# Query order, masks, mixing factors and due offsets in a fused attention and MLP block on one core

## The chip, the core and the metric

The kernel runs on one core of a Trainium2 chip. The time is the device time of one execution in microseconds. The core has five engines that each work through a queue of their own in program order: PE (matrix multiply, with its weight loads shown apart as PEld), DVE (vector), ACT (scalar and activation), POOL (general) and SP, which issues the DMAs here. The engines wait for each other through semaphores.

## The reference

The input has 8 batches of 512 tokens of width 256. Two layers are computed. The first adds an attention and an FP4-quantised MLP to the tokens, both fed with the normalised tokens; the second adds a gated recurrence with its own small MLP and an INT4 linear layer. The change lies in the attention of the first layer, which is, for each of 16 heads of width 64 with 64 memory keys ahead of the 512 keys of the batch:

```python
dots = jnp.einsum('bhid,bhjd->bhij', q, k) * SCALE
dots = jnp.einsum('bhij,hk->bkij', dots, pre_proj)      # heads are mixed before the softmax
dots = jnp.where(causal[None, None], mask_value, dots)
kth = jax.lax.top_k(dots, TOPK)[0][..., -1:]             # TOPK = 64
dots = jnp.where(dots < kth, mask_value, dots)
attn = jax.nn.softmax(dots, axis=-1)
attn = jnp.einsum('bhij,hk->bkij', attn, post_proj)      # and after it
out = jnp.einsum('bhij,bhjd->bhid', attn, v)
```

Everything is fp32.

## The kernel before, in words

The program has three stages. **Preparation** transposes and quantises weights. **Attention** then works through 64 groups: 8 batches of 8 groups of 64 queries. The last part of it also runs the MLP of batch 0 and the quantising of batch 1 (`early_mlp`, `begin_last`). The **second phase** runs the MLP of the other batches and the second layer.

A group g of a batch holds 8 blocks of 8 queries, and a block lies in SBUF with 128 partitions (16 heads by 8 queries) and as many columns as it may see keys, 72 to 576. Groups are taken in the order 7, 0, 5, 2, 6, 1, 4, 3, and two successive groups share one set of queries. The steps of a group are:

- `queries` (L1020), once for a pair: PE multiplies the query weights with the normalised tokens (L1032), four 128 x 128 products to a PSUM bank, each as two passes, so that a half of the pair shows as 16 matmuls. ACT evicts the bank (L1040) and sorts the queries by block on the way, with a write pattern whose neighbouring elements lie four apart.
- `scores` (L1049): in two halves of four blocks each, PE makes raw scores per head (L1066, tiles of 64 x 32), ACT copies them out (L1081), SP issues four DMAs (L1088) that spread them from rows of queries to blocks of heads, PE mixes the heads with the constant `blend` (L1101), ACT takes the exponential (L1109). POOL then multiplies the last 64 columns of all eight blocks with a prepared 0/1 array `reach` (L1118).
- `search` (L1255) finds the 64th largest value of each row by counting: five rounds of eight counts, on ACT (L1144) or DVE (L1148, L1150), and a small step between rounds (`narrow`, L1162) on POOL or DVE. The tables `LONG`, `EDGE` (first two groups) and `LAST` (last four groups) say for each round how many of the eight counts go to ACT and whether the step runs on POOL.
- `soften` (L1294): DVE takes the eight largest below the threshold (L1214, L1217), picks the value (L1221 to L1228) and zeroes what is smaller (L1241). `mixers` (L1318): POOL multiplies the constant `mix` with the reciprocal row sums in two products of 512 elements (L1330).
- `attend` (L1338): PE turns the rows and mixes heads (L1373, L1353), ACT evicts (L1379), PE multiplies with the values (L1397), ACT evicts (L1412). `project_out` (L1418) follows for each pair.

Scores live in one ring of 16,896 columns. `room` (L1445) cuts it into three levels of 5,632; a pair fills a level, one group from its start, one from its end. Six groups are in flight.

The order of work is written out by a planner (`Plan`, L97). Every step is added with an engine, an assumed cost, its dependencies and the buffers that it takes. Each gets a due time from the table `DUE` (L62), as an offset in groups from its own group's place on a nominal clock. `Plan.run` (L130) simulates the engines with the assumed costs and, among steps that could start at about the same moment on an engine, issues the one that is due first. The resulting order is fixed in the program; the chip keeps it per engine, whatever the real durations are. `MLP_DUE` and `BEGIN_DUE` place the early MLP and the early quantising relative to the last group.

In the second phase, tiles live in 16 pieces of 1,024 columns of the ring, listed by number (L1741 to L1744). A branch with an exact version of the attention (L1692) follows the attention and is not taken with these inputs.

Of the kernel before, what the change touches and what calls it, by code (L numbers as in the profile page):

```python
# [32 lines left out]
ORDER = (7, 0, 5, 2, 6, 1, 4, 3)  # L33

RING = 3 * 5632
PACE = 33.0
LEVEL = GB * (WD[0] + WD[-1])
# [12 lines left out]
LAST = ((GB, True),) * 2 + ((GB // 2, False),) * 2 + ((0, False),)  # L50
# [9 lines left out]
MLP_DUE = (-3.18, 3.76)  # L60
BEGIN_DUE = (1.83, 3.43)
DUE = dict(  # L62
    tokens=((-5.94, 2.79),),
    keys=((-7.0, -2.2),),
    queries=((-2.66, -2.56),),
    scores=((-0.82, 0.09), (-0.22, -0.17),),
    search=((2.83, 3.39), (2.51, 3.02),),
    soften=((-1.53, 4.19), (-4.65, -2.79),),
    values=((1.38, 4.78),),
    attend=((5.21, 5.55), (2.0, 2.47),),  # L70
    project=((0.38, 3.82),),
# [560 lines left out]
def block_kernel(ctx: ExitStack, tc: tile.TileContext, a: dict, out: bass.AP):  # L632
# [44 lines left out]
    xqT_1 = piece(15).rearrange("p (e n) -> p e n", e=DC)  # L677
# [3 lines left out]
    with ExitStack() as c0:  # L681
# [16 lines left out]
        reach = keep.tile([P, GB, GR], F32, name="reach")  # L698
# [17 lines left out]
        with tc.tile_pool(name="prep", bufs=1) as prep, tc.tile_pool(name="prep_ps", bufs=1, space=PSUM) as pps:  # L716
# [140 lines left out]
            r.gpsimd.memset(reach, 0.0)  # L857
            for i in range(GB):
                if i:
                    r.gpsimd.memset(reach[:, i, : i * RB], 1.0)  # L860
                r.vector.tensor_scalar(reach[:, i, i * RB : (i + 1) * RB], cmask, -1.0, 1.0, ALU.mult, ALU.add)
# [9 lines left out]
            for c0_, c1_ in ((8192 + DC * 2 * FI, 12288), (12288 + 3 * FI + FKC * D, RING)):  # L871
                r.gpsimd.memset(ring[:, c0_:c1_], 0.0)
# [121 lines left out]
        def keys_of(pl, o, xdone):  # L994
# [3 lines left out]
            for rnd in range(2):  # L998
                for h in range(2):
                    for c in (4 * rnd, 4 * rnd + 2):  # L1000
# [15 lines left out]
                        op = pl.add("PE", 1.9, mm, xdone, ["ps_m"] + ([f"k{rnd}"] if h == 0 and c == 4 * rnd else []), after=[op])  # L1016
# [3 lines left out]
        def queries(pl, pair, o, xdone):  # L1020
# [3 lines left out]
            lo, hi = sorted(pair)  # L1024
            for c0_ in range(0, HC, 4):
                def mm(c0_=c0_):
                    if c0_ == 0:
                        q["T"] = qp_.tile([P, HC, 2, GR], F32, name="qT")
                    q["pq", c0_] = ps = ps_m.tile([P, 512], F32, name="ps_mi")
                    for j in range(4):  # L1030
                        for e in range(DC):
                            nc.tensor.matmul(  # L1032
                                ps[:, j * P : (j + 1) * P].rearrange("p (g i) -> p g i", g=2),
                                wqT[:, e, (c0_ + j) * P : (c0_ + j + 1) * P],
                                o["xnT"][:, e].rearrange("p (g i) -> p g i", i=GR)[:, lo : hi + 1 : hi - lo],
                                start=(e == 0), stop=(e == DC - 1),
                            )

                def evict(c0_=c0_):
                    nc.scalar.copy(  # L1040
                        q["T"][:, c0_ : c0_ + 4].rearrange("p c g (s i b) -> p (c g s) b i", s=2, i=RB),
                        q.pop(("pq", c0_)).rearrange("p (u b i) -> p u b i", b=4, i=RB),
                    )
# [5 lines left out]
        def scores(pl, g, s, q, kdone, qdone, wait=(), free=(), plain=False):  # L1049

            done, raws, op = [], [], None
            side = side_of(g)
            home = pl.add("none", 0.0, lambda: None, wait)
            for sub in range(GR // SUB):
                nk = MEM + g * GR + (sub + 1) * SUB
                k, wires = {}, []
                for rnd in range(2):
                    got = []
                    parts = [(0, nk)] if nk <= 512 else [(0, nk // 2), (nk // 2, nk)]
                    for n0, n1 in parts:  # L1060
                        def mm(rnd=rnd, n0=n0, n1=n1, sub=sub, k=k):
                            k["of", rnd, n0] = some = [ps_m.tile([P, 512], F32, name="ps_mi") for _ in range(2)]
                            for j in range(4):
                                for u in range(2):
# [3 lines left out]
                                        q["T"][rows, 4 * rnd + j, side, sub * SUB : (sub + 1) * SUB],  # L1068
# [4 lines left out]
                            "PE", 0.2 + 0.00166 * (n1 - n0), mm, kdone[rnd] + qdone, ["ps_m"] * 2,  # L1073
# [3 lines left out]
                        for u in range(2):  # L1077
# [5 lines left out]
                            got.append(pl.add("ACT", 0.12 + 0.00083 * (n1 - n0), evict, [op], ["raw"] if n0 == 0 else [], ["ps_m"]))  # L1083
                    for u in range(2):
                        t = 2 * rnd + u

                        def spread(t=t, nk=nk, sub=sub, k=k):
                            nc.sync.dma_start(s[t * SUB : (t + 1) * SUB, 4 * sub : 4 * sub + 4, :nk], k["raw", t][:, :nk])  # L1088
# [3 lines left out]
                        wires.append(pl.add(f"lat{t}", 2.0, lambda: None, [wire], (), ["raw"]))  # L1092
                op2 = None
                for b in range(4 * sub, 4 * sub + 4):
# [11 lines left out]
                    op2 = pl.add("PE", 0.06 * len(cols) + 0.00166 * n, mm, wires, ["ps_s"] * len(cols), after=[op2])  # L1106
                    for i, (n0, n1) in enumerate(cols):
# [5 lines left out]
                        done.append(pl.add("ACT", 0.12 + 0.00083 * (n1 - n0), evict, [op2], (), ["ps_s"]))  # L1113

            def mask():

                at = MEM + g * GR
                nc.gpsimd.tensor_tensor(s[:, :, at:], s[:, :, at:], reach, ALU.mult)  # L1118
                if plain:
                    step = WD[g] + RB  # L1120
                    flat = s.rearrange("p b w -> p (b w)")
                    new = flat[:, at : at + (GB - 1) * step].rearrange("p (b w) -> p b w", w=step)[:, :, :RB]
                    nc.gpsimd.tensor_tensor(new, new, cmask.unsqueeze(1).to_broadcast([P, GB - 1, RB]), ALU.add)
                    new = s[:, GB - 1, WD[g] - RB :]
                    nc.gpsimd.tensor_tensor(new, new, cmask, ALU.add)

            return [pl.add("POOL", 1.1, mask, done)], raws

        def side_of(g):

            return int(g > NG - 1 - g)
# [186 lines left out]
        def mixers(pl, den, w, op=None):  # L1318
# [8 lines left out]
            for j in range(2):  # L1327
                def make(j=j):
                    w["mix"][j] = m = rp.tile([P, 4, P], F32, name="mixd")
                    nc.gpsimd.tensor_tensor(  # L1330
                        m, mix.rearrange("p k i -> p (k i)").unsqueeze(1).to_broadcast([P, 4, P]),
                        w["rden"][:, 4 * j : 4 * j + 4].unsqueeze(2).to_broadcast([P, 4, P]), ALU.mult,
                    )

                done.append(pl.add("POOL", 1.2, make, [op], ["rp"]))
            return done

        def attend(pl, g, s, w, yt, deps, vdone):  # L1338
# [5 lines left out]
            for c, (col, n) in enumerate(chunks):  # L1344
# [22 lines left out]
                for j in range(2 if n == P else 0):  # L1367
# [10 lines left out]
                    def evict(c=c, n=n, j=j):  # L1378
# [6 lines left out]
                        "PE", 0.96, turn, [deps[j]], ["ps_a"] + (["at"] if j == 0 else []),  # L1385
# [5 lines left out]
                def mm(c=c, n=n, last=last):  # L1391
# [12 lines left out]
                    "PE", 1.1, mm, got + vdone, ["ps_y"] if c == 0 else [], ["at"], after=[summed]  # L1404
                )
            side = side_of(g)
            w["turned"] = turned

            def out():
                if side:  # L1410
# [5 lines left out]
            return [pl.add("ACT", 0.5, out, [summed], ["y"] if side else [], ["ps_y"])]  # L1416

        def project_out(pl, dst, pair, yt, deps):  # L1418
# [5 lines left out]
            def add():  # L1424
                out_ = wp.tile([P, D], F32, name="o", bufs=1)
                nc.vector.tensor_tensor(out_, yt.pop("po"), bout, ALU.add)
                for g in pair:
                    nc.sync.dma_start(dst(g), out_[side_of(g) * GR : (side_of(g) + 1) * GR, :])

            op = pl.add("PE", 3.55, mm, deps, ["ps_m"], ["y"])  # L1430
# [14 lines left out]
        def room(n):  # L1445
            g = ORDER[n % NG]
            at = n // 2 % 3 * LEVEL + (LEVEL - GB * WD[g]) * (n % 2)
# [110 lines left out]
        def begin_last(pl, guard, ready):  # L1558
# [4 lines left out]
            def keep_():  # L1563
                nc.sync.dma_start(xq_d, piece(15))
# [10 lines left out]
        groups = [(b, g) for b in range(B) for g in ORDER]  # L1575
# [14 lines left out]

        used = 2 * LEVEL

# [14 lines left out]
        yt, ydone, judged, freed = {}, [], [None, None], []  # L1607
        for n, (b, g) in enumerate(groups):
            if g == ORDER[0]:
# [8 lines left out]
            if n % 2 == 0:  # L1618
                pair = ORDER[n % NG : n % NG + 2]
# [4 lines left out]
            s = room(n)  # L1624
            last = g == ORDER[-1]
# [338 lines left out]
```

## Time and profile before

| | us |
|---|---|
| median of 3 runs (lowest, highest) | 2479.11 (2475.32, 2479.76) |
| the profiled execution | 2485.27 |
| its span | 2483.6 |
| PE busy in the span | 2184.8 |
| DVE busy | 2100.5 |
| ACT busy | 1903.0 |
| POOL busy | 1083.7 |

Busy is the time in which an engine runs an instruction. A group of the profile is written as line, engine, operation, output and inputs with their sizes, then after a bar the busy time in us, the mean duration of one in ns, and the idle time of the engine before them with what ended it. Successive records of one engine may overlap by about 0.1 us, as the end of a matmul or an ACT instruction reaches into the next. In the rows of 40 slices a digit is the busy share of a slice of 62 us in tenths.

### The profile page before, as it was taken

The page shows a single profiled execution, that of the slowest core. Times are in us where ns is not written, and L with a number is a line of the kernel's source. Part 1 is how long each engine was busy: PE and PEld are TensorE (multiplying, and loading weights), DVE is VectorE, ACT ScalarE, POOL GpSimd, SP SyncE. Part 2 cuts the span into 40 slices and gives each one's busy share as a digit, 9 for nine tenths or more (in the row PEclk, how much of TensorE's full clock was granted, in tenths as well). Part 3 has the DMA queues.
Part 4 walks back from the last instruction along what each step waited for, and adds up shares of the span by engine and source line. Part 5 has one row for each costly group of instructions (what it writes and reads, how often), then busy time and mean ns, then how long its engine had stood idle before and what let it go on. Part 6 is the DMA issues. An engine that isn't in the chain of part 4 may idle for free. (4 is left out here: it accounts for less than half of the span.)

```text
span 2483.6 us, 56595 instructions
## 1 busy us (share of the span) xinstructions
PE 2184.8 (88%) x19593; PEld 1546.0 (62%) x19593; DVE 2100.5 (85%) x6550; ACT 1903.0 (77%) x5426; POOL 1083.7 (44%) x2007
## 2 busy tenths in 40 slices
PE   5887999999999998999999999999466789989997
PEld 4544765777677676676767667666355456666654
DVE  8658889998999998999989998899997788777762
ACT  3389989989999999999999999899733446443442
POOL 5103536445454553554545455454424544444330
PEclk8897999999999999999999999999787889999998
DMA  6252242234233225323332422442000310000000
GB/s 221 57 102 44 55 67 47 59 57 71 55 53 70 48 55 78 55 60 57 64 56 48 80 48 61 66 86 64 3 16 16 113 34 25 19 9 18 0 9 17
DMA packets 112222, 134.35 MB, mean 54 GB/s; under 512 B 19356, under 2 KB 97975, under 8 KB 111415
## 3 DMA queue, kind: packets, MB, share of 16 engines
q1 hardware_dynamic: 111926, 130.65, 25.7%
q8 instruction: 156, 2.56, 0.5%
q14 instruction: 140, 1.14, 0.2%
HBM read 27.32 MB, written 15.73 MB: 17 GB/s over the span
## 5 line engine op out<-in xcount | busy, mean ns | idle before, releaser
L1144 ACT ACTIVATE junk<-ring,cur 128x328 int8<-128x328 f32 (+22 forms) x1520 | 856.0, 573 | 10.0 <-POOL cur L1206 5.4
L1148 DVE TENSOR_SCALAR_CACHE_REDUCE junk<-ring,cur 128x520 int8<-128x520 f32 (+7 forms) x976 | 509.1, 540 | 60.7 <-POOL cur L1206 51.3
L1373 PE MATMUL ps_at<-mixd,ring 128*128 128x128 f32 x2560 | 358.6, 291 | 72.4 <-POOL mixd L1330 66.2
L1373 PEld LDWEIGHTS ps_at<-mixd,ring 128*128 128x128 f32 x2560 | 320.9, 200 | 110.5 <-POOL mixd L1330 74.2
L1101 PE MATMUL ps_sc<-ring,blend 128*128 128x276 f32 (+49 forms) x1152 | 358.8, 432 | 24.1 <-DMA ring<-raw 15.1
L1214 DVE SCALAR_TENSOR_TENSOR y<-ring,cur 128x520 f32<-128x520 f32 (+56 forms) x512 | 323.3, 631 | 6.2
L1144 ACT ACTIVATION_READ_ACCUMULATOR junk<-ring,cur 128x1 f32 x1520 | 311.1, 205 | 0.0
L1241 DVE SCALAR_TENSOR_TENSOR ring<-ring,kth 128x520 f32<-128x520 f32 (+56 forms) x512 | 294.0, 582 | 0.9
L1101 PEld LDWEIGHTS ps_sc<-ring,blend 128*128 128x128 f32 x1152 | 191.8, 192 | 155.9 <-ACT ring L1109 73.3
L1160 POOL TENSOR_TENSOR cur<-base,raw 128x8 f32<-128x8 f32 x182 | 44.2, 243 | 537.1 <-ACT junk L1144 508.7
L1217 DVE MAX8 top<-y 128x8 f32<-128x520 f32 (+56 forms) x512 | 255.7, 499 | 17.6
L1109 ACT ACTIVATE ring<-ps_sc 128x280 f32<-128x280 f32 (+33 forms) x576 | 223.5, 416 | 26.7 <-PE ps_sc L1101 20.5
L1397 PE MATMUL ps_y<-at,v 128*64 128x64 f32 (+1 forms) x6144 | 221.3, 225 | 25.5 <-ACT at L1379 19.2
L1397 PEld LDWEIGHTS ps_y<-at,v 128*64 128x64 f32 (+1 forms) x6144 | 196.1, 138 | 74.6 <-ACT at L1379 40.2
L1081 ACT COPY raw<-ps_mi 128x288 f32<-128x288 f32 (+14 forms) x576 | 217.0, 415 | 29.5 <-DMA ring<-raw 19.0
L1066 PE MATMUL ps_mi<-kt,qT 64*32 64x288 f32 (+14 forms) x4608 | 227.1, 428 | 12.3 <-ACT raw L1081 11.4
L1379 ACT COPY at<-ps_at 128x512 f32<-128x512 f32 x320 | 188.9, 595 | 38.6 <-PE ps_at L1373 36.3
L1196 POOL TENSOR_TENSOR by<-gap,minus 128x8 f32<-128x8 f32 x120 | 204.9, 1707 | 9.4
L1330 POOL TENSOR_TENSOR mixd<-mix,rden 128x512 f32<-128x512 f32 x128 | 142.6, 1129 | 101.4 <-DVE rden L1322 49.2
L1118 POOL TENSOR_TENSOR ring<-ring,reach 128x512 f32<-128x512 f32 x64 | 86.4, 1350 | 197.6 <-ACT ring L1109 113.0
L260 PE MATMUL ps_gu<-big,ring 128*128 128x352 f32 x448 | 149.7, 480 | 16.6 <-DVE hid L260 10.3
L1422 PE MATMUL ps_mi<-woT,y 128*128 128x256 f32 x512 | 131.0, 414 | 16.2 <-ACT y L1412 16.2
(308 smaller groups left out, 3954.7 us busy)
## 6 DMA issues: line engine op xcount, KB each, us to landing
ring<-raw SPq DMA_DIRECT2D x32, 288.0 KB
ring<-raw SPq DMA_DIRECT2D x32, 272.0 KB
ring<-raw SPq DMA_DIRECT2D x32, 256.0 KB
ring<-raw SPq DMA_DIRECT2D x32, 240.0 KB
ring<-raw SPq DMA_DIRECT2D x32, 224.0 KB
ring<-raw SPq DMA_DIRECT2D x32, 208.0 KB
ring<-raw SPq DMA_DIRECT2D x32, 192.0 KB
ring<-raw SPq DMA_DIRECT2D x32, 176.0 KB
```

The lines of the kernel that those rows point to most:

```text
L1066: nc.tensor.matmul(some[u][j * SUB : (j + 1) * SUB, : n1 - n0], q["T"][rows, 4 * rnd + j, side, sub * SUB : (sub + 1) * SUB], kt[rows, 4 * ...
L1081: nc.scalar.copy(k["raw", 2 * rnd + u][:, n0:n1], k["of", rnd, n0][u][:, : n1 - n0])
L1101: nc.tensor.matmul(ps[:, : n1 - n0], blend.rearrange("p k i -> p (k i)"), s[:, b, n0:n1], start=True, stop=True,)
L1109: nc.scalar.activation(s[:, b, n0:n1], k["pb", b][i][:, : n1 - n0], AF.Copy if plain else AF.Exp, scale=DH ** -0.5)
L1144: nc.scalar.activation(junk, src, AF.Sign, bias=thr, scale=-1.0, accum_out=raw[:, b : b + 1])
L1148: nc.vector.tensor_scalar(junk, src, thr, 0.0, ALU.is_ge, ALU.add, accum_out=raw[:, b : b + 1])
L1196: eng.tensor_tensor(by, gap[:, 1], minus, ALU.pow)
L1214: nc.vector.scalar_tensor_tensor(y, src, cur[:, 0, b : b + 1], src, ALU.is_lt, ALU.mult)
L1217: nc.vector.max(out=top[:, b, 1:], in_=y)
L1241: nc.vector.scalar_tensor_tensor(src, src, kth[:, b : b + 1], e, ALU.is_ge, ALU.mult, accum_out=den[:, b : b + 1])
L1373: nc.tensor.matmul(pt[:n, b * P : (b + 1) * P], s[:, 4 * j + b, col : col + n], w["mix"][j][:, b, :], start=True, stop=True,)
L1397: nc.tensor.matmul(w["py"][j * DH : (j + 1) * DH, q * GR : (q + 1) * GR], vs[c][:n, k * DH : (k + 1) * DH], ats[c][:n, k, :], start=(c == ...
```

## The change

- **Queries.** The moving operand of L1032 is read query by query across the blocks, with a step of 8 columns, so the PSUM bank already holds the sorted order and the eviction is a plain copy.
- **Halves.** The first half of a group's scores takes blocks 0, 2, 4, 6 and the second 1, 3, 5, 7, so the first half is 24 columns wider than before. The query weights of the raw scores are read with a step of 2.
- **Masks.** `reach` is gone. For each half POOL clears the columns behind each block's last key with memsets (four and three), once the DMAs have landed, and after the exponentials multiplies only the 8 newest columns of the blocks by an 8-column array `below` (two products). The memsets of unused parts of the ring in the preparation go.
- **Mixing factors.** The two products of 512 elements become four of 256.
- **Ring.** `places` lays groups first in, first out, and lists for each group the earlier ones that it overlaps; those are waited for.
- **Planner.** All due offsets change, and several assumed costs.
- **Last groups.** `LAST` gives all counts of rounds three and four to ACT, and the step after round three to POOL.
- **Later pieces.** The pieces of the second phase are numbered by when the last groups free them, and the early quantising waits for the groups that lie where it writes.

```diff
+ORDERS = (ORDER,) * B
-LEVEL = GB * (WD[0] + WD[-1])
+SCRATCH = 11264
+def places(order):
+    at, found, held = 0, [], [(-1, SCRATCH, RING)]
+    for n, g in enumerate(order):
+        size = GB * WD[g]
+        if at + size > RING:
+            at = 0
+        found.append((at, [m for m, c0, c1 in held if c0 < at + size and at < c1]))
+        held = [(m, c0, c1) for m, c0, c1 in held if not (at <= c0 and c1 <= at + size)] + [(n, at, at + size)]
+        at += size
+    return found, held
-LAST = ((GB, True),) * 2 + ((GB // 2, False),) * 2 + ((0, False),)
+LAST = ((GB, True),) * 3 + ((GB, False), (0, False))
-MLP_DUE = (-3.18, 3.76)
-BEGIN_DUE = (1.83, 3.43)
+MLP_DUE = (-5.1, -4.84)
+BEGIN_DUE = (-0.86, 4.46)
 DUE = dict(
-    tokens=((-5.94, 2.79),),
-    keys=((-7.0, -2.2),),
-    queries=((-2.66, -2.56),),
-    scores=((-0.82, 0.09), (-0.22, -0.17),),
-    search=((2.83, 3.39), (2.51, 3.02),),
-    soften=((-1.53, 4.19), (-4.65, -2.79),),
-    values=((1.38, 4.78),),
-    attend=((5.21, 5.55), (2.0, 2.47),),
-    project=((0.38, 3.82),),
+    tokens=((-6.23, -2.15),),
+    keys=((-3.1, 0.28),),
+    queries=((-1.77, -0.35),),
+    scores=((-0.29, 0.89), (0.36, 0.78),),
+    search=((2.42, 5.15), (3.63, 5.17),),
+    soften=((1.27, 3.95), (0.74, 2.19),),
+    values=((4.79, 5.02),),
+    attend=((6.0, 6.0), (-2.66, 5.66),),
+    project=((-3.36, 2.98),),
...
@@ queries
                             nc.tensor.matmul(
-                                ps[:, j * P : (j + 1) * P].rearrange("p (g i) -> p g i", g=2),
-                                wqT[:, e, (c0_ + j) * P : (c0_ + j + 1) * P],
-                                o["xnT"][:, e].rearrange("p (g i) -> p g i", i=GR)[:, lo : hi + 1 : hi - lo],
+                                ps[:, j * P : (j + 1) * P], wqT[:, e, (c0_ + j) * P : (c0_ + j + 1) * P],
+                                o["xnT"][:, e].rearrange("p (g b i) -> p g i b", b=GB, i=RB)[:, lo : hi + 1 : hi - lo],
                                 start=(e == 0), stop=(e == DC - 1),
                             )
...
-                    nc.scalar.copy(
-                        q["T"][:, c0_ : c0_ + 4].rearrange("p c g (s i b) -> p (c g s) b i", s=2, i=RB),
-                        q.pop(("pq", c0_)).rearrange("p (u b i) -> p u b i", b=4, i=RB),
-                    )
+                    nc.scalar.copy(q["T"][:, c0_ : c0_ + 4].rearrange("p c g i -> p (c g i)"), q.pop(("pq", c0_)))
@@ scores
-                nk = MEM + g * GR + (sub + 1) * SUB
+                nk = keys(g * GB + GB - 2 + sub)
...
-                                        q["T"][rows, 4 * rnd + j, side, sub * SUB : (sub + 1) * SUB],
+                                        q["T"][rows, 4 * rnd + j, side, sub::2],
...
-                            nc.sync.dma_start(s[t * SUB : (t + 1) * SUB, 4 * sub : 4 * sub + 4, :nk], k["raw", t][:, :nk])
+                            nc.sync.dma_start(s[t * SUB : (t + 1) * SUB, sub::2, :nk], k["raw", t][:, :nk])
...
+                def clear(sub=sub):
+                    for b in range(sub, GB - 1, 2):
+                        nc.gpsimd.memset(s[:, b, keys(g * GB + b) :], 0.0)
+
+                done.append(pl.add("POOL", 0.7, clear, wires))
...
-                nc.gpsimd.tensor_tensor(s[:, :, at:], s[:, :, at:], reach, ALU.mult)
+                by, op = (cmask, ALU.add) if plain else (below, ALU.mult)
+                nc.gpsimd.tensor_tensor(new, new, by.unsqueeze(1).to_broadcast([P, GB - 1, RB]), op)
+                new = s[:, GB - 1, WD[g] - RB :]
+                nc.gpsimd.tensor_tensor(new, new, by, op)
@@ mixers
-                    nc.gpsimd.tensor_tensor(
-                        m, mix.rearrange("p k i -> p (k i)").unsqueeze(1).to_broadcast([P, 4, P]),
-                        w["rden"][:, 4 * j : 4 * j + 4].unsqueeze(2).to_broadcast([P, 4, P]), ALU.mult,
-                    )
+                        nc.gpsimd.tensor_tensor(
+                            w["mix"][j][:, 2 * h : 2 * h + 2],
+                            mix.rearrange("p k i -> p (k i)").unsqueeze(1).to_broadcast([P, 2, P]),
+                            w["rden"][:, 4 * j + 2 * h : 4 * j + 2 * h + 2].unsqueeze(2).to_broadcast([P, 2, P]), ALU.mult,
+                        )
@@ assumed costs in us, n columns
-keys PE 1.9; raw scores PE 0.2 + 0.00166 n; score evictions ACT 0.12 + 0.00083 n; turn PE 0.96; values PE 1.1; project PE 3.55
+keys PE 1.8; raw scores PE 0.28 + 0.00166 n; score evictions ACT 0.05 + 0.00083 n; turn PE 1.05; values PE 1.15; project PE 3.7
@@ the guard of the early quantising
-            if n == len(groups) - 5:
-                guard = pl.add("none", 0.0, lambda: None, ydone[-1:])
+        guard = [freed[m] for m, c0, c1 in held if c0 < (homes[2] + 1) * 1024 and homes[2] * 1024 < c1]
+        guard = pl.add("none", 0.0, lambda: None, guard)
```

The assumed costs are shown in one line each; in the code they stand in the calls to `pl.add`. The mixing of heads in `scores` also gets 0.04 us more.

## The prediction

> **What bounds the kernel now.** I read the page first, then the busy times by stage.
>
> ```profile
> span 2483.6 us, 56595 instructions
> ...
> PE   5887999999999998999999999999466789989997
> DVE  8658889998999998999989998899997788777762
> ACT  3389989989999999999999999899733446443442
> ```
>
> Slices 4 to 27 (about 200 to 1,740 us) are the attention groups: PE, DVE and ACT are all near full. From slice 28 ACT empties, DVE stays full for about 160 us, and then the second phase runs on PE. Two neighbouring batches and that full DVE stretch, from the view by stages (PE, weight loads, DVE, ACT, POOL; then clock, DMA share, GB/s):
>
> ```profile
> 835.80:1044.00 208.20, 198.77 (x2178) 143.45 (x2177) 189.44 (x667) 200.80 (x617) 102.95 (x223) 0.98 0.34 60
> 1044.00:1252.40 208.40, 198.89 (x2178) 143.51 (x2177) 189.46 (x669) 200.93 (x618) 102.75 (x223) 0.98 0.33 60
> 1740.00:1900.00 160.00, 88.78 (x784) 71.02 (x782) 153.10 (x499) 76.40 (x214) 56.49 (x75) 0.78 0.03 8
> ```
>
> One batch of eight groups takes 208.3 us. PE is busy for 198.8 of it and ACT for 200.9, so each idles some 8 to 9 us: whatever adds PE time adds nearly that much to the batch, while relief on one of the two alone buys little. The waits in these two batches show no hidden reserve on PE; those for the turned factors and for the mixing factors are a few microseconds, and the long ones are POOL's own (total us, times, longest):
>
> ```profile
> POOL cur L1160 <- ACT junk L1144: 135.4, 34, 11.9
> ...
> PEld ps_y L1397 <- ACT at L1379: 10.7, 14, 1.2
> ...
> PEld ps_at L1373 <- POOL mixd L1330: 4.4, 6, 1.0
> ```
>
> **Part 1, the query order.** L1032 streams the normalised tokens as moving operand, now in runs of 64 neighbouring elements; the change steps 8 floats (32 bytes) from element to element. The eviction (L1040), which now does the reordering, becomes a plain copy.
>
> ```profile
> 1002.29 1.95 PE L1032 MATMUL ps_mi<-xnT,big 128*128 128x128 f32 x16
> 1004.08 0.86 PE L1101 MATMUL ps_sc<-ring,blend 128*128 128x200 f32 x4
> ```
>
> Sixteen matmuls from 1002.29 to the next start at 1004.08 are 112 ns each, 0.87 ns a column. No strided moving operand stands in the trace. The nearest rows are the same kind of step on other engines. First the eviction, which writes at a 16-byte step, against contiguous copies (groups of the two batches; after the bar busy us and mean ns):
>
> ```profile
> L1040 ACT COPY qT<-ps_mi 128x512 f32<-128x512 f32 x16 | 17.4, 1120 | 0.1
> ...
> L1081 ACT COPY raw<-ps_mi 128x512 f32<-128x512 f32 x8 | 4.4, 583 | 0.0
> ...
> L1081 ACT COPY raw<-ps_mi 128x96 f32<-128x96 f32 x8 | 1.8, 245 | 2.7 <-DMA ring<-raw 2.7
> ```
>
> Then DVE in the preparation, reading the identity at a 32-byte step, against a contiguous reduction of 128 elements (shortest/median/longest ns):
>
> ```profile
> L260 DVE TENSOR_REDUCE row<-ident x1: 383/383/383, 2.0 to 2.0; 128x8 f32<-128x128 f32 x1
> ...
> L260 DVE TENSOR_REDUCE sq<-each_head x2: 285/287/289, 66.9 to 67.8; 128x16 f32<-128x128 f32 x2
> ```
>
> The two L1081 forms give ACT (583 - 245) / 416 = 0.81 ns an element; the strided eviction pays 537 ns more over 512, so 1.86 ns. [...] A batch has 128 of them (4 pairs, 2 halves, 16): **+15.1 us of PE a batch**. Bounds: 0 if the matmul stream hides the step; +350 ns (44.8 us a batch) if it fetches every float twice, once for each of its two array passes. A gain is excluded, as nothing is shortened on PE. I take the rows. On ACT the eviction falls from 1120 to 583 ns: 8 a batch, **-4.3 us of ACT**.
>
> **Part 2, interleaved blocks.** The two halves of a group now hold blocks 0,2,4,6 and 1,3,5,7, so the first half's raw scores are 24 columns wider. PE: two rounds, two passes of 24 x 0.87 ns, 84 ns a group, +0.7 us a batch. ACT: four copies x 24 x 0.81 = 78 ns a group, +0.6 us a batch. SP issues the same four DMAs per half, each 12 KB longer; the DMA engines are a third busy. [...]
>
> **Part 3, POOL.** The 512-element mask product becomes seven memsets and two 8-wide products; two mixing products become four of 256.
>
> ```profile
> L1330 POOL TENSOR_TENSOR mixd<-mix,rden 128x512 f32<-128x512 f32 x32 | 35.6, 1126 | 33.0 <-DVE rden L1322 18.0 <-PE ps_at L1373 8.7 <-PE ps_at L1353 6.3
> L1118 POOL TENSOR_TENSOR ring<-ring,reach 128x512 f32<-128x512 f32 x16 | 21.7, 1356 | 18.3 <-ACT ring L1109 17.4 <-issue 0.3 <-DMA ring<-raw 0.2
> L1160 POOL TENSOR_TENSOR cur<-base,raw 128x8 f32<-128x8 f32 x48 | 11.5, 240 | 135.6 <-ACT junk L1144 135.4
> ```
>
> And from the preparation, memsets by shape:
>
> ```profile
> L260 POOL MEMSET reach<- 128x56 f32 x1 | 0.1, 150 | 0.0
> ...
> L260 POOL MEMSET reach<- 128x8 f32 x1 | 0.1, 110 | 0.0
> ```
>
> Memsets of 8 to 56 columns at 110 to 150 ns: seven are 0.91 us. The products, from 240 ns at 8 elements and 1126 at 512 (1.76 ns an element): 0.33 + 0.24. So 1.48 us against 1.36, and 0.57 us instead of 1.36 between the last exponential and the search. Mixing: 4 x 0.68 against 2 x 1.13, +0.45 us. POOL gains 0.6 us a group, 5 us a batch, beside 105 idle: 0. Without that cover each memset run would cost its 0.4 to 0.5 us. The memsets wait for the score DMAs to land; behind them in POOL's queue stand the search steps (ten products, L1160 to L1206), for which ACT's and DVE's next counts wait, and the mixing factors, for which L1373 waits. The old mask product waited later still, for the exponentials. I take 0, bounds -0.5 to +1 us a group.
>
> **Part 4, ring, dues, planner costs.** Each pair of groups fills 5632 columns, so first-in-first-out puts every group where it already lies, and its waits are those of the overlapping groups. No instruction, 0. The new due offsets only reorder. PE's 9.5 idle us a batch are what a better order could win and, doubled, what a worse one could cost: +-9 us a batch; I take 0, since no row prefers an order. The planner still counts 2.0 us for a half of the queries, which by part 1 takes 3.7; what is late next is the score rounds behind it on PE.
>
> **Part 5, the end.** For the last four groups eight DVE counts each go to ACT and one search step from DVE to POOL.
>
> ```profile
> L1150 DVE SCALAR_TENSOR_TENSOR junk<-ring,cur,two 128x488 int8<-128x488 f32 (+15 forms) x32 | 25.2, 798 | 0.0
> ```
>
> DVE loses 25 us of counts and four steps of nine instructions at 0.2 us, 7 us, where it is busy for 153 of 160 us. But a round of eight counts in a row on ACT (0.55 + 0.19 us each, some 5 us) and a POOL step (ten products, 5.0 us from 1008.4 to 1013.4 in the view in order of time) is slower than the split round, and the early MLP's new due puts it ahead of the same groups, with a tail that nothing covers. Take -18, bounds -32 and +10. The prepared mask and ring memsets (3.5 us of POOL) vanish behind the first loads: 0. Batch 1's early quantising now waits for the turn of the 59th group instead of the 60th's output, and the last phase does the same work in other pieces of the ring; PE and DVE are set by the amount of work in both, so 0.
>
> **The sum**, against the profiled 2485.3 us (span 2483.6, 1.7 around it; 6.2 above the median of 2479.1). PE per batch 198.8 + 15.1 + 0.7 = 214.6. ACT falls to 197 and DVE stays at 189, so PE alone is the bound and I let half of its 9.5 idle stay: 219.4, +11.1 a batch, +89 in eight (50 with no idle left, 126 with all of it). With -18: +71, 2556 on the profiled run, **2550 us** against the median, 2.9% slower. Its own range, with +-25 for order and end: 2505 to 2605.
>
> **Rivals.**
> *The step is hidden, and it gets faster.* [...] PE +0.7, ACT -3.7 a batch with the same idle gives about -2.5, -20 in eight, -18 at the end: 2441. Between this and my case lie 109 us for 118 ns, so it decides below some 41 ns extra a matmul.
> *The order.* The step is hidden, but the dues make PE wait for mixing factors or scores: each us of idle a batch is 8 us, from 5 us on it eats the gain; doubled idle gives 2441 + 76 = 2517. For it: waits of 20 us already stand in the last groups; against it: only single ones before them.
> *Two fetches a float.* 214.6 + 29.7 with half the idle is +41 a batch, about 2790. Nothing in the trace doubles so.
> *Nothing to see.* A price near 41 ns cancels the gains: 2479.
>
> **How the numbers follow.** My case 0.68, hidden 0.19, order 0.07, two fetches 0.03, cancelled 0.03. 0.2% (5 us) is about what a measurement of this kernel tells from no change. The hidden case spans 2400 to 2474; holding 8 in 10 needs most of my case and part of it: 2430 to 2610. Slower 0.77, same 0.04, faster 0.19.
>
> **What would show it.** L1032's successor starting 16 at some 230 ns apart and 30 us a batch busy where 15.9 are now; the query eviction at 583 ns; batches of about 219 us with ACT and DVE under 92%. Matmuls still 112 ns apart and batches under 208 us would prove me wrong.

## The result and the profile after

The changed kernel takes 2533.2 us (median of 4 runs, 2530.3 to 2536.2) against 2478.4 for the kernel before (4 runs, 2475.3 to 2479.8): a ratio of 1.0223, 95% interval 1.0205 to 1.0241. It is slower, as forecast, by 55 us where 71 were forecast (2533 against 2550), and inside both ranges that the prediction gave.

The page of the changed kernel, the same rows as before:

```profile
span 2529.1 us, 57360 instructions
...
PE   4888989999999999999999999999777788999997
DVE  8558878897888889788888978879789698877672
ACT  3379978989998998999899899888973355444442
```

PE is at nine tenths or more in 28 slices, as many as before, and DVE and ACT have stepped back: one engine binds the attention now. The same engines in two batches and in a stretch of 160 us in which the last groups end (stages view, columns as before):

```profile
866.50:1084.50 218.00, 211.58 (x2177) 152.91 (x2176) 184.82 (x668) 197.68 (x616) 104.21 (x302) 1.00 0.33 59
1084.50:1303.80 219.30, 212.37 (x2177) 153.06 (x2176) 185.16 (x667) 197.87 (x616) 104.16 (x302) 1.00 0.32 59
1800.00:1960.00 160.00, 113.24 (x1065) 89.39 (x1064) 146.03 (x457) 105.49 (x310) 77.85 (x151) 0.85 0.07 17
```

A batch takes 218.7 us instead of 208.3, and PE is busy for 212.0 of it instead of 198.8. Where those 13 us come from is seen in the order of time: the query matmuls (now L1045) and what starts after them.

```profile
1030.31 3.89 PE L1045 MATMUL ps_mi<-xnT,big 128*128 128x128 f32 x16
1034.02 0.85 PE L1116 MATMUL ps_sc<-ring,blend 128*128 128x400 f32 x2
```

Sixteen matmuls take 3.71 us to the next start, 232 ns each; before it was 1.79 us and 112 ns. The groups of the two batches show the rest of the list (busy us, mean ns, idle before):

```profile
L1052 ACT COPY qT<-ps_mi 128x512 f32<-128x512 f32 x16 | 9.3, 584 | 21.4 <-PE ps_mi L1045 21.4
...
L1343 POOL TENSOR_TENSOR mixd<-mix,rden 128x256 f32<-128x256 f32 x64 | 41.4, 674 | 16.1 <-DVE rden L1332 13.1 <-PE ps_at L1388 1.6 <-PE ps_at L1368 1.4
...
L1137 POOL TENSOR_TENSOR ring<-ring,below 128x56 f32<-128x56 f32 x16 | 5.1, 320 | 33.2 <-ACT ring L1124 33.2
...
L1105 POOL MEMSET ring<- 128x56 f32 x16 | 2.3, 144 | 28.7 <-DMA ring<-raw 28.7
```

The eviction of the queries fell from 1120 to 584 ns, and ACT now waits for the queries' matmuls instead: 21.4 us in these two batches.

The two profiled executions (2485.3 and 2530.8 us) differ by 45.5 us, 9 us less than the medians, mainly because the one of the kernel before was 7 us above its median. In the table, the marks are the first DVE product of each group's pick (L1223 in the kernel before), which all programs issue once per group:

| stretch | before, us | after, us | difference |
|---|---|---|---|
| start to the pick of group 1 | 204.1 | 207.1 | +3.0 |
| seven batches, picks 1 to 57 | 1465.1 | 1531.1 | +66.0 |
| pick 57 to pick 64 | 223.5 | 205.6 | -17.9 |
| pick 64 to the end | 590.9 | 585.3 | -5.6 |

### The profile page after: what moved, and what is told of

It reads as the page before. It is cut to its first block, busy times and chain, and to the rows that moved or that the text cites. A ratio compares the mean times of both kernels' runs of the same rounds, so it can differ in the third digit from the quotient of the medians.

```text
span 2529.1 us, 57360 instructions
## 1 busy us (share of the span) xinstructions
PE 2291.5 (91%) x19593; PEld 1615.3 (64%) x19593; DVE 2025.3 (80%) x6443; ACT 1892.3 (75%) x5490; POOL 1103.2 (44%) x2677
## 5 line engine op out<-in xcount | busy, mean ns | idle before, releaser
L1154 ACT ACTIVATE junk<-ring,cur 128x392 int8<-128x392 f32 (+36 forms) x1552 | 888.4, 588 | 10.9 <-POOL cur L1189 6.3
L1116 PE MATMUL ps_sc<-ring,blend 128*128 128x264 f32 (+50 forms) x1152 | 363.1, 436 | 42.4 <-DMA ring<-raw 25.8
L1154 ACT ACTIVATION_READ_ACCUMULATOR junk<-ring,cur 128x1 f32 x1552 | 342.3, 221 | 0.0
L1124 ACT ACTIVATE ring<-ps_sc 128x272 f32<-128x272 f32 (+33 forms) x576 | 236.7, 435 | 48.3 <-PE ps_sc L1116 45.0
L1227 DVE MAX8 top<-y 128x8 f32<-128x520 f32 (+56 forms) x512 | 255.7, 499 | 17.6
L1090 ACT COPY raw<-ps_mi 128x284 f32<-128x284 f32 (+15 forms) x576 | 229.2, 440 | 38.8 <-PE ps_mi L1075 16.5
L1045 PE MATMUL ps_mi<-xnT,big 128*128 128x128 f32 x1024 | 251.6, 414 | 1.0 <-ACT raw L1090 0.9
L1075 PE MATMUL ps_mi<-kt,qT 64*32 64x284 f32 (+15 forms) x4608 | 236.9, 437 | 10.1 <-ACT raw L1090 8.4
L1045 PEld LDWEIGHTS ps_mi<-xnT,big 128*128 128x128 f32 x1024 | 208.3, 206 | 40.2 <-issue 5.5
L1412 PE MATMUL ps_y<-at,v 128*64 128x64 f32 (+1 forms) x6144 | 219.4, 225 | 12.4 <-ACT at L1394 7.5
L1343 POOL TENSOR_TENSOR mixd<-mix,rden 128x256 f32<-128x256 f32 x256 | 165.1, 672 | 69.6 <-DVE rden L1332 35.9
L1105 POOL MEMSET ring<- 128x56 f32 (+6 forms) x448 | 34.6, 124 | 345.5 <-DMA ring<-raw 340.2
```

What stands on the lines that cost most here:

```text
L1045: nc.tensor.matmul(ps[:, j * P : (j + 1) * P], wqT[:, e, (c0_ + j) * P : (c0_ + j + 1) * P], o["xnT"][:, e].rearrange("p (g b i) -> p g i ...
L1075: nc.tensor.matmul(some[u][j * SUB : (j + 1) * SUB, : n1 - n0], q["T"][rows, 4 * rnd + j, side, sub::2], kt[rows, 4 * rnd + j, n0:n1], sta ...
L1116: nc.tensor.matmul(ps[:, : n1 - n0], blend.rearrange("p k i -> p (k i)"), s[:, b, n0:n1], start=True, stop=True,)
L1124: nc.scalar.activation(s[:, b, n0:n1], k["pb", b][i][:, : n1 - n0], AF.Copy if plain else AF.Exp, scale=DH ** -0.5)
L1154: nc.scalar.activation(junk, src, AF.Sign, bias=thr, scale=-1.0, accum_out=raw[:, b : b + 1])
L1227: nc.vector.max(out=top[:, b, 1:], in_=y)
```

## The experiments

Ratios are to the kernel before, measured beside the runs; its median there was 2479.6 to 2480.8 us.

**The query order alone.** The kernel before, with the change's moving operand. To leave everything behind it as it was, the eviction is two copies of 256 elements (382 ns each, so ACT has 2.8 us less a batch than before). The planner's costs are untouched, and in the trace PE, DVE and POOL run the same instructions in the same order as before.

```diff
-    ps[:, j * P : (j + 1) * P].rearrange("p (g i) -> p g i", g=2), wqT[...],
-    o["xnT"][:, e].rearrange("p (g i) -> p g i", i=GR)[:, lo : hi + 1 : hi - lo],
+    ps[:, j * P : (j + 1) * P], wqT[...],
+    o["xnT"][:, e].rearrange("p (g b i) -> p g i b", b=GB, i=RB)[:, lo : hi + 1 : hi - lo],
...
+    for half in range(2):
+        nc.scalar.copy(to[:, :, half], ps[:, :, half])
```

> The kernel before with the 32-byte step of the queries' moving operand alone; the eviction is two contiguous-read copies of 256 elements that write runs of four, so that everything behind it stays as it was. Theory S (the step halves the matmul stream and PE passes it on): query matmuls 232 ns apart, batches of 208.3 us become 218 to 220, time 2478 + 75 to 90, about 2560, since the gain of the last groups is missing. Rival O (the step is absorbed in PE's 9.5 idle us a batch and the other due offsets made the kernel slower): matmuls 232 ns apart, but batches under 211 us and 2478 to 2500.

2581.9 us, ratio 1.0412 (1.0386 to 1.0437): 102 us, more than the whole change costs, and 22 more than the 2560 expected. The matmuls stand 233 ns apart. Batches take 221.2 us (mean of seven), and PE, in one of them, is again the engine that fills it:

```profile
1106.60:1327.90 221.30, 211.96 (x2177) 153.91 (x2176) 191.38 (x667) 199.58 (x624) 101.50 (x223) 0.99 0.31 56
```

PE keeps some 9 us of idle time, as before. The first pick comes at 220.6 us instead of 204.1, so the start, which the expectation had left out, pays 16 us as well: in the trace a whole batch's query matmuls stand ahead of that pick. The rival that PE's idle time would absorb the step falls.

**The query order undone.** The changed kernel with the contiguous moving operand; the eviction sorts, writing with a step of 8.

```diff
-    o["xnT"][:, e].rearrange("p (g b i) -> p g i b", b=GB, i=RB)[:, lo : hi + 1 : hi - lo],
+    o["xnT"][:, e].rearrange("p (g i) -> p g i", i=GR)[:, lo : hi + 1 : hi - lo],
...
+    q["T"][:, c0_ : c0_ + 4].rearrange("p c g (i b) -> p (c g) b i", i=RB),
+    q.pop(("pq", c0_)).rearrange("p (u b i) -> p u b i", b=GB, i=RB),
```

> The changed kernel with the contiguous moving operand back and the sorting in the eviction (which now writes with a 32-byte step, expected at 1.1 us). Theory S: matmuls 112 ns apart, batches of 206 to 209 us, time 2533 minus 70 to 90, about 2455, faster than the kernel before by the gain of the last groups. Rival O: still slower than the kernel before, 2500 or more.

2457.4 us, ratio 0.9916 (0.9892 to 0.9941). Matmuls are 111 ns apart again, the batches 209.7 us. Undoing this one part turns the change from 2.2% slower to 0.8% faster: 76 us. All other parts together, in this company, gain 23 us. PE, DVE, ACT and POOL run the same instructions in the same order in both traces, so the 76 us are those of the step and of the eviction that goes with it (ACT has 4 us a batch more again), and not of another order. Without the step PE idles 11.7 us a batch, with it 6.7, where the kernel before kept its idle time.

**What a step costs.** A kernel that only runs short series on one core and leaves the whole computation out: 24 matmuls or copies for each pattern.

```python
x.rearrange("p (n k) -> p n k", k=k)[:, :128, 0]          # step k
x.rearrange("p (n k) -> p n k", k=8)[:, : 128 // r, :r]   # runs of r neighbours every 8
```

> Only short series, the outputs are left out (zeros). fp32 matmuls of 128 columns, moving operand with steps of 1, 2, 4, 8, 16 elements, then runs of 2 and of 4 neighbours every 8; then the stationary operand with steps 2, 4, 8; then ACT copies of 512 elements from PSUM: contiguous, writing with steps 4 and 8, reading PSUM with steps 8 and 8 (written contiguously), and an SBUF read with step 8. [...] Rival (a price for every non-contiguous pattern): step 2 and the runs also above 150 ns. PSUM reads with a step: open, 590 if PSUM has no such price on ACT, 1100 if it has.

Every fp32 matmul stands as two records, so 24 matmuls are 48 records; busy time over 48 is about the spacing. The lines are for the moving operand with steps of 1, 2, 4 and 8 (L64, L66, L68, L70), runs of 2 and 4 every 8 (L74, L76), and the stationary operand with steps of 2 and 4 (L78, L80); then ACT: contiguous (L85), writing with step 8 (L89), reading PSUM with step 8 (L93), reading SBUF with step 8 (L95).

```profile
L95 ACT COPY to<-x 128x512 f32<-128x512 f32 x24 | 26.6, 1107 | 0.8
L89 ACT COPY to<-pb 128x512 f32<-128x512 f32 x24 | 25.8, 1073 | 0.8
...
L93 ACT COPY to<-pb 128x512 f32<-128x512 f32 x24 | 14.1, 586 | 0.8
L85 ACT COPY to<-pb 128x512 f32<-128x512 f32 x24 | 14.1, 586 | 99.8 <-PE pb L83 99.1
...
L70 PE MATMUL ps<-x,ident 128*128 128x128 f32 x48 | 11.4, 412 | 0.0
L80 PE MATMUL ps<-x 128*128 128x128 f32 x48 | 11.4, 397 | 0.0
...
L68 PE MATMUL ps<-x,ident 128*128 128x128 f32 x48 | 11.0, 405 | 0.0
...
L78 PE MATMUL ps<-x 128*128 128x128 f32 x48 | 5.8, 281 | 0.0
...
L74 PE MATMUL ps<-x,ident 128*128 128x128 f32 x48 | 5.7, 278 | 0.0
L66 PE MATMUL ps<-x,ident 128*128 128x128 f32 x48 | 5.6, 274 | 0.0
L64 PE MATMUL ps<-x,ident 128*128 128x128 f32 x48 | 5.5, 275 | 0.0
...
L76 PE MATMUL ps<-x,ident 128*128 128x128 f32 x48 | 5.5, 275 | 0.0
```

Steps of 4 and 8 floats double the stream (11.0 and 11.4 us against 5.5; start to start 226 and 233 ns against 112), and a step of 16 takes about as much (218 ns). A step of 2, and runs of 2 or of 4 neighbours, cost next to nothing (112 to 116 ns). So not every non-contiguous pattern is dear: the three series with a single float every 4, 8 or 16 pay, those with a float every 2 and with pairs or fours every 8 do not. The stationary operand shows the same (118 ns with a step of 2, 233 with 4). On ACT a step of 8 nearly doubles a copy, from 586 ns to 1073 where it writes SBUF and to 1107 where it reads it, and costs nothing when it reads PSUM (586). All of this is fp32; other types were not run.

**The sorting on the reading side.** That last line gives a third place for it, open to both kernels: the matmul contiguous, and the eviction turned so that it walks PSUM with the step and writes SBUF in order.

```diff
-    q["T"][:, c0_ : c0_ + 4].rearrange("p c g (s i b) -> p (c g s) b i", s=2, i=RB),
-    q.pop(("pq", c0_)).rearrange("p (u b i) -> p u b i", b=4, i=RB),
+    q["T"][:, c0_ : c0_ + 4].rearrange("p c g (s i b) -> p (c g s) i b", s=2, i=RB),
+    q.pop(("pq", c0_)).rearrange("p (u b i) -> p u i b", b=4, i=RB),
```

In the changed kernel (with 8 blocks in place of 2 x 4):

> The changed kernel with the contiguous moving operand, and the sorting done by the eviction on its reading side: it reads PSUM with a step of 8 and writes SBUF contiguously. By the short series this costs ACT 586 ns instead of 1105 and PE 112 ns a matmul. If ACT and PE bind together: ACT has 4.2 us less a batch than in the run with the order undone, batches of 206 to 208 us, about 2440. If PE alone binds: no gain over that run, 2457.

In the kernel before:

> The kernel before with the eviction alone turned: it reads PSUM with a step and writes contiguously. L1040 at 586 ns instead of 1120. If ACT and PE bind together: batches fall by 2 to 3 us, 2480 - 20 = 2460. If PE alone binds: 2475 to 2483.

2439.8 us, ratio 0.9838 (0.9820 to 0.9857), and 2460.9 us, ratio 0.9933 (0.9909 to 0.9958). The eviction in the changed kernel, with the order undone and then turned:

```profile
L1053 ACT COPY qT<-ps_mi 128x512 f32<-128x512 f32 x16 | 17.4, 1088 | 3.4 <-PE ps_mi L1045 3.2
```

```profile
L1053 ACT COPY qT<-ps_mi 128x512 f32<-128x512 f32 x16 | 9.3, 578 | 2.8 <-PE ps_mi L1045 2.7
```

In both kernels PE, DVE, ACT and POOL keep their order of instructions, so only this eviction's time differs. Four microseconds of ACT a batch are worth 17.6 and 19.9 us of the whole, 2.5 and 2.8 over each of seven batches (in the kernel before, the batches after the first fall from 208.4 to 205.6): ACT binds beside PE where PE does not carry the step. The first of the two is the fastest kernel of this study, 1.6% below the kernel before and 3.7% below the changed one. The changed kernel's eviction takes as long (584 ns), so the 93 us between these two are the price of the matmul's step alone in this order. The stages of the fastest kernel are read from its profiled execution, which took 2453.3 us against 2439.4 to 2440.0 in the other four.

**LAST alone, and with the turned eviction.**

```diff
-LAST = ((GB, True),) * 2 + ((GB // 2, False),) * 2 + ((0, False),)
+LAST = ((GB, True),) * 3 + ((GB, False), (0, False))
```

> The kernel before with the new table LAST alone. If the counts taken from DVE make the shorter end (theory S's -18): the stretch from the pick of the fourth group from the end of batch 7 to the last pick shortens by 15 to 25 us, time about 2460. If the new due offsets of the early MLP made it: no gain, 2475 to 2490, because eight counts in a row on ACT lengthen each round.

> The kernel before with the turned eviction and the new table LAST. The two are in different stretches, so the gains should add: the run with the turned eviction alone minus 12 us, about 2448. If the batches' gain is lost at the end, no better than LAST alone, 2468.

2467.7 us, ratio 0.9948 (0.9930 to 0.9967): 12.6 us less, where 20 were expected. The stretch from pick 57 to pick 64 falls from 223.5 to 207.3 us. The four last groups keep DVE for less of it (compare 153 of 160 us before):

```profile
1740.00:1880.00 140.00, 86.14 (x776) 69.26 (x776) 124.09 (x377) 90.57 (x268) 66.26 (x112) 0.79 0.03 9
```

Together with the turned eviction it is 2447.0 us, ratio 0.9877 (0.9853 to 0.9901): 2480.8 less 19.9 and 12.6 would make 2448.3, so the two add.

**The due offsets.** First all of the new ones with LAST in the kernel before, then all of the old ones in the changed kernel (contiguous operand, turned eviction), then the two of the early MLP alone, in the kernel before with the turned eviction and LAST.

```diff
-MLP_DUE = (-3.18, 3.76)
-BEGIN_DUE = (1.83, 3.43)
-DUE = dict(...)   # as in the kernel before
+MLP_DUE = (-5.1, -4.84)
+BEGIN_DUE = (-0.86, 4.46)
+DUE = dict(...)   # as in the changed kernel
```

> The kernel before with the new due offsets (DUE, MLP_DUE, BEGIN_DUE) and LAST, nothing else; the assumed costs stay. If the dues give what the run with the order undone has over LAST alone: 2457, with the first pick near 195 us. If masks, interleaved halves, mixing in four and the costs give it: 2468 or slower, because these dues were not made for this kernel's steps.

> The changed kernel with the contiguous moving operand and the turned eviction, but with all due offsets of the kernel before. Fourth corner beside the new steps with new dues (2440), old steps with old dues (2447 with LAST) and old steps with new dues (2562, order in the eviction as before). If each set of dues fits only the steps it stands with: 2480 or more. If the old dues are simply better: 2430 to 2440.

> The kernel before with the turned eviction, LAST, and the new MLP_DUE and BEGIN_DUE, which put the early MLP ahead of the last groups; the other due offsets stay. If the early MLP's place gives part of the shorter end: under 2440, with the last write of the early MLP earlier than 1880 us. If it only takes DVE from the last groups: 2447 or more.

| steps | old dues | new dues |
|---|---|---|
| of the kernel before, with LAST | 2467.7 | 2562.0, ratio 1.0333 (1.0313 to 1.0353) |
| of the changed kernel, eviction turned | 2519.2, ratio 1.0159 (1.0133 to 1.0185) | 2439.8 |

Each set fits only the steps, and the planner's assumed costs for them, that it stands with: crossing them costs 94 us in one kernel and 79 in the other. The dues add no instruction; the loss is idle time and, on PE, clock. In 1,200 us of the attention, the kernel before and then the same steps with the new dues and LAST:

```profile
420.00:1620.00 1200.00, 1141.36 (x12553) 824.70 (x12552) 1091.63 (x3847) 1149.02 (x3509) 584.52 (x1261) 0.98 0.33 60
```

```profile
420.00:1620.00 1200.00, 1071.82 (x11551) 768.14 (x11550) 1035.86 (x3641) 1083.31 (x3298) 554.46 (x1191) 0.96 0.30 55
```

PE, DVE and ACT all lose together, 70, 56 and 66 us: they wait for each other, and no engine is full. PE's granted clock (third number from the right) also falls, from 0.98 to 0.96. Two of these waits, from two batches of the kernel before:

```profile
DVE junk L1148 <- POOL cur L1206: 10.9, 7, 2.6
...
PE ps_at L1373 <- POOL mixd L1330: 2.8, 4, 0.8
```

and from two batches of the second kernel:

```profile
DVE junk L1148 <- POOL cur L1206: 31.1, 9, 9.3
...
PE ps_at L1373 <- POOL mixd L1330: 16.8, 1, 16.8
```

The two offsets of the early MLP and the early quantising alone change nothing that can be measured: 2444.5 us, ratio 0.9873 (0.9846 to 0.9899), against 2447.0. They hardly move the early MLP either: its last write comes at 1882.8 us instead of 1879.4. Picks 57 to 64 take 211.4 us instead of 208.0, and what follows takes 585.5 instead of 596.3, so it is the last pick that shifts. What another place of the early MLP would be worth was therefore not tested.

**The planner's cost put right.** In the changed kernel, a half of the queries counts what it takes.

```diff
-op = pl.add("PE", 2.0, mm, xdone, ["ps_m"] + (["q"] if c0_ == 0 else []), after=[op])
+op = pl.add("PE", 3.7, mm, xdone, ["ps_m"] + (["q"] if c0_ == 0 else []), after=[op])
```

> The changed kernel with one number of the planner put right: a half of the queries counts 3.7 us on PE instead of 2.0, so the order is made for what the step really costs. If PE's time itself is what the batches pay: 2533 within 10 us, batches near 218. If the wrongly planned order is part of the price (rival): batches of 213 or less, under 2505.

2537.3 us, ratio 1.0236 (1.0213 to 1.0260). Seven batches take 218.6 us in the mean, as before the correction. Planning with the true time wins nothing back, so the price of the step is PE's time. (The due offsets stayed as they were; a set made for the true time was not tried.)

**Mixing factors in two products again**, in the fastest kernel (four products of 256 replaced by two of 512).

```diff
-    for h in range(2): nc.gpsimd.tensor_tensor(w["mix"][j][:, 2 * h : 2 * h + 2], ...)
+    nc.gpsimd.tensor_tensor(w["mix"][j], ...)
```

> The changed kernel with the contiguous moving operand and the turned eviction, and the mixing factors in two products of 512 again (1.1 us each instead of 2 x 0.67). If the four parts cost nothing because POOL is half idle (as predicted): 2440 within 8 us. If the split factors let POOL's search steps in earlier and this matters: 2450 or more.

2473.6 us, ratio 0.9977 (0.9967 to 0.9987), 34 us more than with four parts. It was expected to be free, or 2450 and more if the split mattered. POOL does less work, and the batches swing between 205 and 220 us. This doesn't say that smaller products are worth 34 us: with one step in place of two the planner wrote a different order, and about a third of PE's runs of like matmuls stand in another place than in the fastest kernel. In 1,200 us of the attention PE waits for the mixing factors for 0.9 us with four parts and 1.0 us with two, so a direct wait for the larger products does not show. Split and order were not separated, so the cause stays open.

## Why the prediction was right

**The step of the moving operand, right.** No row or run from before the result shows the term of +15.1 us a batch, 118 ns a matmul; it was the author's estimate, carried over to PE from rows of ACT and DVE. What the runs showed in its place: 232 to 233 ns a matmul against 112, and in the changed kernel PE's busy time for the queries rose from 15.87 to 31.46 us a batch, +15.6. On DVE the rows come to much the same price as ACT's 1.86 ns an element: its counts (L1148) rise in two batches of the kernel before from 276 ns at 72 columns to 806 at 576, 1.05 ns a column, and the 96 ns by which the two reductions of L260 differ are 0.75 ns more over 128 elements, together 1.80. For PE it was an analogy with no row of PE behind it; the short series showed it afterwards (226 to 233 ns with steps of 4 and 8). The eviction came to 584 ns (583).

**The hidden step** (19%) is excluded by 232 ns; so are two fetches a float, which at the forecast +350 ns would have made about 460.

**Interleaved blocks, small as forecast.** The raw scores take 1.2 us of PE more a batch (227.1 to 236.9 us in the whole run) where 0.7 stood. Their stationary operand, the queries read with a step of 2, loads as fast as before (105 and 106 ns).

**POOL, right in its parts and in costing nothing.** Memsets take 104 to 144 ns (110 to 150 forecast), products 320 and 245 (324 and 240), mixing 674 (680). POOL's busy time in a batch rose from 102.9 to 104.2 us, where 5 more were forecast, beside over 100 idle. In the changed kernel POOL stands waiting for landing DMAs ahead of the memsets, 64 us in the two batches, but PE's idle time did not grow (9.5 to 6.7 us a batch).

**The sum of a batch, right by two errors that cancel, which is luck.** PE was put at 214.6 us busy and half of its idle, 4.7, on top: 219.4. It came to 212.0 and 6.7: 218.7. "Half" had no row behind it: with the order alone all of the idle time stayed. The other work of PE fell by 2.4 us although its scores grew, and the prediction had no such term. The granted clock rose from 0.98 to 1.00 (see the end), but with the step undone it was 1.00 too, and PE's other work was only 1.2 us lower than in the kernel before; the rest stays open.

**Eight batches, too much.** The term that was mis-sized is "+89 in eight". Between the first picks of batches 1 and 8 lie seven batches, and they grew by 9.4 us each in the mean, 66 (the two shown grew by 10.4; the mean is lower, as the first of the kernel before took 215.0). Batch 8's queries are all made before its first pick, and a batch's worth of them before the first of all, so the eighth share falls into the start. There the changed kernel shows only +3. That is two things: without the step the changed kernel comes to the first pick earlier than the kernel before (195.4 us with the order undone, 202.6 with the turned eviction, against 204.1), and the step takes 5 to 12 back (207.1). Over the whole, undoing the order of the queries measures what it costs here: 76 us, not 89; all the rest gains 21 to 23, where 18 were forecast.

**The end, right in size.** -18 was forecast; it was -17.9 from pick 57 to pick 64 and -5.6 after. The -18 was an estimate between bounds of -32 and +10, so that it fits to the tenth is luck. LAST alone gives -12.6 on the median of the whole, so it is the larger part. That the early MLP would come ahead of the last groups did not happen: its first matmul comes 117 us after pick 57 in the changed kernel and 104 in the kernel before.

**The order, wrong as a term.** "I take 0, bounds +-9 us a batch" held for the change as a whole, but the reasoning did not: dues cannot be judged apart from the steps. Crossed with the wrong steps they cost 12 us a batch in the kernel before (208.5 with LAST to 220.7), more than the bound.

**"Relief on one of the two alone buys little"** was half right: 4.3 us of ACT a batch bought 2.5 to 2.8. The rival of the hidden step used 2.5. (ACT's idle time before was 7.4 us a batch, not the 8 to 9 read; nothing rests on it.)

## What to carry to other kernels

Ask of each strided operand what its step costs, for matmul operands too, and measure it in a short series: here, in fp32, a single float every 4 or 8 doubled the matmul stream (226 and 233 ns against 112), while pairs of neighbours every 8 cost next to nothing (116 ns at most). If data have to be sorted, do it where the step is free, here in a copy's reading of PSUM (586 ns with the step and without), and keep it off the engine that binds. Where an order is planned and fixed, a change of steps has to be judged together with the planner's settings: swapping either alone cost 79 to 94 us here, about as much as the order that was under test (76 to 102).

## What the hardware showed beyond that

This is about PE's clock. In the kernel before, five of the seven batches between first picks had two stretches of 3.4 us at half the clock. PE's work ahead of one of them shows three short waits in a row (start, duration, in brackets the idle time and what ended it):

```profile
1142.06 1.15 PE L1397 MATMUL ps_y<-at,v 128*64 128x64 f32 x32 [0.81 <-ACT at L1379]
...
1145.13 1.15 PE L1397 MATMUL ps_y<-at,v 128*64 128x64 f32 x32 [0.83 <-ACT at L1379]
1147.68 4.54 PE L1422 MATMUL ps_mi<-woT,y 128*128 128x256 f32 x12 [1.39 <-ACT y L1412]
```

The stages around it (PE busy is the first number after the length, the granted clock the third from the right):

```profile
1140.00:1144.00 4.00, 3.19 (x51) 2.93 (x50) 3.90 (x10) 4.00 (x14) 2.06 (x6) 1.00 1.06 131
1144.00:1148.00 4.00, 1.78 (x37) 1.42 (x36) 3.66 (x19) 3.97 (x11) 2.89 (x8) 1.00 0.25 31
1148.00:1151.50 3.50, 3.50 (x10) 2.79 (x9) 3.06 (x14) 3.50 (x13) 0.00 (x0) 0.51 0.00 0
1151.50:1156.00 4.50, 4.50 (x48) 2.85 (x46) 2.88 (x10) 4.08 (x12) 0.00 (x0) 1.00 0.12 29
```

None of the waits was longer than 1.4 us, PE was busy for 1.8 of the 4 us before 1148, and the next 3.5 us ran at 0.51. That the waits brought on the half clock is not shown: no run changed them alone. What it costs is: the 16 matmuls of L1422 from 1147.68 take 5.24 us to the next start, at 1152.92, and the 16 from 1091.87, at a clock of 1.00, took 3.45. Two such stretches a batch cost about 3.4 us of work (an estimate: half of 2 x 3.4 us). The changed kernel ran at a clock of 1.00 through the 1,200 us that were shown for the due offsets, and so did the one with the order undone:

```profile
420.00:1620.00 1200.00, 1164.89 (x11874) 836.50 (x11868) 1016.95 (x3667) 1090.21 (x3397) 578.65 (x1668) 1.00 0.32 59
```

```profile
420.00:1620.00 1200.00, 1136.35 (x12550) 814.45 (x12548) 1055.62 (x3827) 1140.56 (x3517) 601.65 (x1718) 1.00 0.34 62
```

So the clock of 1.00 does not come from the step's added work alone: without the step PE is busy for 1136 us, less than the 1141 of the kernel before, and the clock is 1.00 all the same. The step alone in the kernel before gave 0.99, the new dues with the old steps 0.96, the old dues with the new steps 0.98. What in the changed kernel goes with 1.00 was not separated. In the stretch shown, the 1.8 us of the half clock are paid on top of the idle time.
